# Steps of two batches in a fused attention kernel: one run of small matmuls for a pair's scores and the preceding pair's values

## The chip, the core and the metric

The kernel runs on one core of one Trainium2 chip. The metric is the device time of one execution in microseconds (us); a time of the kernel is the median of several executions. In the profile the engines are PE (TensorE: matmuls; PEld is its loading of weights), DVE (VectorE), ACT (ScalarE), POOL (GpSimd) and SP (SyncE, which issues the DMAs).

## What is computed

The input x has 64 batches of 128 tokens of 512 values, all in float32. The output is x plus an attention block of x:

```python
xn = layernorm(x, g_in)
q = (xn @ Wq).reshape(b, n, H, DH).transpose(0, 2, 1, 3) * scale   # H = 16, DH = 64
k, v = split(xn @ Wkv)                # one key and one value head for all 16 query heads
k, v = one null key and null value ahead of the 128
sim = einsum('bhid,bjd->bhij', q, k) + bias      # a bias for each head, query and key
sim = where(causal_mask, neg, sim); sim = where(mask, sim, neg)
attn = softmax(sim)
out = einsum('bhij,bjd->bhid', attn, v) -> (b, n, 1024)
return x + layernorm(out @ Wo, g_out)
```

## The kernel before, in words

Each engine executes its instructions strictly in the order in which the program writes them (a manual schedule); the order of the calls in the step functions is the order on every engine. An engine that waits at one instruction holds up all behind it.

**Tokens and queries.** Batches come in groups of four (GB). load_x brings a tile of tokens, norm_stats (L265 to L270) takes its mean and variance on DVE and a power on POOL, norm_nmr (L278) one more scalar on DVE, norm_apply (L291) normalizes on ACT; it calls norm_nmr itself, so that scalar stands in DVE's order where norm_apply is called. tokens_T (L315) transposes in blocks on DVE, tokens_out (L324) and tokens_in (L332) send the group through memory into xT. The queries of a group are made by Strassen's scheme: token_sum (L460, POOL) forms four sums of token halves, weight_sum four of weights; for each of four query tiles f, product(g, f, 1) to product(g, f, 7) (L478) do four matmuls each with 256 columns (two instructions a matmul) into PSUM tiles "a", "c" (pool ps_q) and "w" (ps_w). keep (L489) copies a partial sum out of "a" on ACT before the next product is added to it, q_out (L496 on ACT, L499 on DVE) writes a quarter of the queries to qT. kv_mm (L343) and kv_out (L364) make keys and values of a batch; keys_T (L388) and values_spread lay them out by DMA once for each group.

**Attention of a batch.** bias_add (L516, POOL) makes the tile S with bias and mask. The queries are in two halves: the upper 64 see at most 64 keys, the lower 64 see 128. scores (L548) does 64x64 matmuls for a half, scores_add (L564 for two split tiles, L566 for a whole one) adds them to S on DVE, scores_max (L571) takes row maxima on DVE, exps (L580) exponentiates on ACT with the sums of each row, rinv (L597) is a reciprocal on DVE, scale (L601) multiplies on POOL, blocks_T (L616) transposes 32x32 blocks on DVE. values (L645) does 32x64 matmuls, values_out (L662) copies them on ACT to oT.

**Output.** out_mm (L676) multiplies a batch's oT with Wo: eight matmuls of 512 columns. For 28 pairs of batches (1, 2) to (55, 56) Strassen's scheme takes its place: out_sums (L709 to L712) makes four sums on POOL, out_product 1 to 7 (L729) four matmuls each of 256 columns, with copies (out_keep, L741 on DVE and L743 on ACT) and sums (out_part, L750 on ACT and L752 on DVE). The layer norm of a batch is then pair_stats (L758 to L762), pair_pow (L766, POOL), pair_nmr (L773), pair_norm (L783, ACT, into PSUM tile "Y"), pair_gain (L786), pair_residual (L789) and store. Batches outside the pairs (0 and 57 to 63) use out_mm, out_stats and residual.

**Steps.** step(n) is one batch: step_a for even n, step_b for odd n, then region(n), in which PE does the small matmuls: scores of batch n + 2 and values of batch n. Between two regions PE does full-array work: one query tile (seven products), keys and values of one batch, and three or four output products. Queries are made six batches ahead. last_step takes the batches from n = 58 on, which have no more queries to make.

Of the kernel before, what the change touches and what calls it, by code (L numbers as in the profile page):

```python
# [17 lines left out]
def kernel(  # L18
# [113 lines left out]

    def load_res_pair(n):
        for b in (n - 2, n - 1):
            if 1 <= b and not plain(b):
                load_res(b)
# [221 lines left out]
    kvts, vds = {}, {}  # L358

    def kv_out(m, pkv):  # L360
        g, t = divmod(m, GB)
        if t == 0:
            kvts[g] = hp.tile([P, 2, GB, DH], FP, tag="kv", name=f"kvt_{g}", bufs=1)
# [6 lines left out]
        if t == GB - 1:  # L370
            vds[g] = dp.tile([P, GB * DH], FP, tag="vd", name=f"vd_{g}")
            to_tokens(vds[g], kvts[g][:, 1].rearrange("p t d -> p (t d)"))
# [12 lines left out]
    def keys_T(g):  # L385
# [8 lines left out]
        kT[g] = hp.tile([P, NQ, GB, Q], FP, tag="kT", name=f"kT_{g}")  # L394
# [19 lines left out]
    def q_tile(g):  # L414
        qT[g] = gp.tile([P, NF, GB, 2, 2, DH], FP, tag="qT", name=f"qT_{g}")

    def q_part(g, c, lo=0, hi=GB):

        return qT[g][:, c % NF, lo:hi, :, c // NF, :]

    def q_half(c, h):
        if c == 0 and h == 0:
            q_tile(0)
        pq = ps_q.tile([P, HT], FP, tag="ac"[c % 2], name=f"pq_{c}_{h}")
        two = slice(2 * h, 2 * h + 2)
        for kc in (2, 0, 3, 1):
# [8 lines left out]
            q_part(0, c, two.start, two.stop),  # L435
# [55 lines left out]
    def q_out(g, c, toks, tag, name=None):  # L491
        lo = toks.start // N
        o = q_part(g, c, lo, lo + 2)
# [32 lines left out]
    def lower_home(n):  # L526

        tiles = [
            ps_y.tile([P, HE], FP, tag="Y", name=f"lo0_{n}"),
            ps_w.tile([P, HE], FP, tag="w", name=f"lo1_{n}"),  # L530
        ]
        return [t.rearrange("p (f j) -> p f j", f=NF) for t in tiles]

    def scores(b, hf, home=None):
        g, t = divmod(b, GB)
        nk = N if hf == 1 else NL
        split = home is not None
        if not split:
            ps = ps_s.tile([P, 2, NF, N], FP, tag="s", name=f"ps_{b}_{hf}")
            pv = ps.rearrange("p r f j -> p r (f j)")[:, :, 0 : NF * nk].rearrange(  # L540
                "p r (f j) -> p r f j", f=NF
            )
            home = [pv[:, r] for r in range(2)]
        for f in range(NF):
            for r in range(2):
                rows = slice(r * DH, (r + 1) * DH)
                for u in range(2):
                    nc.tensor.matmul(  # L548
                        home[r][u * DH : (u + 1) * DH, f, :],
                        qT[g][rows, f, t, hf, u],  # L550
# [4 lines left out]
        pss[b, hf] = home if split else pv  # L555
# [763 lines left out]
```

## Time and profile before

| | |
|---|---|
| median of 3 executions | 1074.78 us |
| lowest, highest | 1074.32, 1075.43 us |
| the profiled execution | 1079.76 us |
| its span in the profile | 1078.0 us |
| granted clock of TensorE, mean | 0.998 |
| DMA traffic | 105.14 MB, mean 98 GB/s |

The profile shows one execution. A span is the time from its first to its last instruction, and times in rows count from the span's start. In a row of the order of time, the first number is the start in us, the second the time until the end of the last of the xN merged instructions, then engine, line, operation, output tile <- input tiles and shapes; in brackets the idle time of the engine just before it and what ended it. The durations of matmuls overlap (the array is a pipeline), so the spacing of the starts tells more than the durations.

### The profile page before, as it was taken

The page shows a single profiled execution, that of the slowest core. Times are in us where ns is not written, and L with a number is a line of the kernel's source. Part 1 is how long each engine was busy: PE and PEld are TensorE (multiplying, and loading weights), DVE is VectorE, ACT ScalarE, POOL GpSimd, SP SyncE. Part 2 cuts the span into 40 slices and gives each one's busy share as a digit, 9 for nine tenths or more (in the row PEclk, how much of TensorE's full clock was granted, in tenths as well). Part 3 has the DMA queues.
Part 4 walks back from the last instruction along what each step waited for, and adds up shares of the span by engine and source line. Part 5 has one row for each costly group of instructions (what it writes and reads, how often), then busy time and mean ns, then how long its engine had stood idle before and what let it go on. Part 6 is the DMA issues. An engine that isn't in the chain of part 4 may idle for free.

```text
span 1078.0 us, 31342 instructions
## 1 busy us (share of the span) xinstructions
PE 1055.6 (98%) x12292; PEld 884.2 (82%) x12292; DVE 771.3 (72%) x1572; ACT 703.9 (65%) x2826; POOL 702.9 (65%) x520
## 2 busy tenths in 40 slices
PE   7989999999999999999999999999999999999997
PEld 7776888888888888888888888888888888888543
DVE  4767677777777777777777778777777777656772
ACT  3446676676676676676676667667667667657681
POOL 3666767586675767667586675768667576766562
PEclk9999999999999999999999999999999999999999
DMA  6414323423134332323423233341422432211211
GB/s 203 148 38 128 118 82 97 138 73 116 62 99 137 97 109 71 120 84 97 138 79 117 66 120 104 97 136 55 128 71 92 143 97 89 71 41 45 66 60 69
DMA packets 69076, 105.14 MB, mean 98 GB/s; under 512 B 9536, under 2 KB 33728, under 8 KB 67136
## 3 DMA queue, kind: packets, MB, share of 16 engines
q1 hardware_dynamic: 68112, 102.08, 29.9%
q8 instruction: 97, 1.59, 0.6%
q10 hardware_dynamic: 816, 1.05, 0.3%
q14 instruction: 51, 0.42, 0.1%
HBM read 67.45 MB, written 35.65 MB: 96 GB/s over the span
## 4 chain that ended last, share of the span: by engine, by line
PE 91%; DVE 2%; POOL 2%; DMA 2%; ACT 2%; issue 1%; ACTq 0%; SPq 0%; DVEq 0%; POOLq 0%
PE pa L478 19%; PE pyX L729 18%; PE pc L478 10%; PE pyY L729 9%; PE po L645 7%; PE pkv L343 6%; PE ps L548 5%; PE pw L478 5%; PE pyw L729 4%; PE lo L548 3%; PE py L676 3%; PE pq L427 1%; DMA x<-in_x_dram 1%; ACT s L580 1%; POOL s L516 1%
## 5 line engine op out<-in xcount | busy, mean ns | idle before, releaser
L580 ACT ACTIVATE s<-s,nmax 128x65 f32<-128x65 f32 (+1 forms) x1024 | 373.3, 373 | 4.2 <-DVE nmax L571 4.2
L601 POOL TENSOR_TENSOR s<-s,rinv 128x512 f32<-128x512 f32 (+1 forms) x128 | 189.5, 1481 | 178.1 <-DVE rinv L597 171.3
L516 POOL TENSOR_TENSOR s<-biasp,mneg 128x1552 f32<-128x1552 f32 x64 | 206.9, 3233 | 72.6 <-DVE sb L616 69.4
L580 ACT ACTIVATION_READ_ACCUMULATOR s<-s,nmax 128x1 f32 x1024 | 200.9, 196 | 0.0
L662 ACT ACTIVATE oT<-po,nv 128x256 f32<-128x256 f32 x256 | 100.6, 475 | 150.3 <-PE po L645 150.3
L729 PE MATMUL pyX<-wT,oT 128*128 128x256 f32 x672 | 161.7, 383 | 0.0
L729 PEld LDWEIGHTS pyX<-wT,oT 128*128 128x128 f32 x672 | 125.4, 190 | 20.7 <-issue 4.8
L478 PE MATMUL pa<-xS,wq 128*128 128x256 f32 x480 | 123.5, 380 | 1.0 <-ACT ku L489 1.0
L571 DVE TENSOR_REDUCE nmax<-s 128x8 f32<-128x520 f32 (+1 forms) x128 | 122.5, 957 | 2.3
L616 DVE STREAM_TRANSPOSE sb<-s 128x1536 f32<-128x1536 f32 x64 | 113.3, 1770 | 6.6 <-PE po L645 4.3
L478 PEld LDWEIGHTS pa<-xS,wq 128*128 128x128 f32 x480 | 90.9, 190 | 14.2 <-ACT ku L489 1.8
L645 PE MATMUL po<-sb,vr 32*64 32x128 f32 (+1 forms) x4096 | 92.0, 305 | 2.0 <-issue 2.0
L489 ACT COPY ku<-pa 128x256 f32<-128x256 f32 x120 | 44.7, 373 | 70.5 <-PE pa L478 65.5
L645 PEld LDWEIGHTS po<-sb,vr 32*64 32x64 f32 x4096 | 71.1, 130 | 18.2 <-issue 12.2
L566 DVE TENSOR_TENSOR s<-ps,s 128x1024 f32<-128x1024 f32 (+1 forms) x70 | 81.7, 1167 | 2.8 <-PE ps L548 2.7
L709 POOL TENSOR_TENSOR yS<-oT 128x512 f32<-128x512 f32 x28 | 35.7, 1275 | 71.1 <-ACT oT L662 71.1
L564 DVE TENSOR_TENSOR s<-lo,s 128x256 f32<-128x256 f32 x116 | 43.8, 420 | 47.8 <-PE lo L548 47.7
L548 PE MATMUL ps<-kT,qT 64*64 64x128 f32 (+1 forms) x2240 | 72.2, 266 | 1.9 <-DVE s L566 1.9
L343 PE MATMUL pkv<-wkv,xT 128*128 128x128 f32 x512 | 70.4, 281 | 3.5 <-ACT xT L304 2.7
L343 PEld LDWEIGHTS pkv<-wkv,xT 128*128 128x128 f32 x512 | 64.3, 191 | 11.5 <-issue 4.6
L499 DVE TENSOR_TENSOR qT<-pc,ku 128x256 f32<-128x256 f32 x120 | 49.4, 412 | 25.2 <-ACT ku L489 19.0
L291 ACT ACTIVATE x<-x,nmr,rstd 128x512 f32<-128x512 f32 x60 | 48.7, 814 | 28.1 <-DVE nmr L278 25.7
(99 smaller groups left out, 2061.4 us busy)
## 6 DMA issues: line engine op xcount, KB each, us to landing
x<-in_x_dram SPq DMA_DIRECT2D x64, 256.0 KB
res<-in_x_dram SPq DMA_DIRECT2D x64, 256.0 KB
out_dram<-y SPq DMA_DIRECT2D x64, 256.0 KB
xd<-xb SPq DMA_DIRECT2D x14, 1024.0 KB
xT<-xd SPq DMA_DIRECT2D x56, 256.0 KB
vr<-vd SPq DMA_DIRECT2D x64, 128.0 KB
kT<-kd SPq DMA_DIRECT2D x64, 64.0 KB
wo<-in_L_cond_Wo_dram SPq DMA_DIRECT2D x1, 2048.0 KB
```

Source lines behind the costliest of these rows:

```text
L343: nc.tensor.matmul(pkv, xT[g][:, t, kc, :], wkv[:, kc, :], start=(kc == 0), stop=(kc == KC - 1),)
L478: nc.tensor.matmul(prod[tag], w[:, kc, f * P : (f + 1) * P], t[:, :, kc, :], start=(start and kc == 0), stop=(kc == HK - 1), skip_group_ch ...
L516: nc.gpsimd.tensor_tensor(S[b], biasp, mneg[:, t].unsqueeze(1).broadcast_to([P, R8, ROW]), ALU.add,)
L548: nc.tensor.matmul(home[r][u * DH : (u + 1) * DH, f, :], qT[g][rows, f, t, hf, u], kT[g][rows, 0 : nk // Q, t, :], start=True, stop=True,)
L566: nc.vector.tensor_tensor(sv, pv, sv, ALU.add)
L571: nc.vector.tensor_reduce(nmax[b][:, hf], S[b][:, :, WITH_NULL[hf]], AX.X, ALU.max, negate=True)
L580: nc.scalar.activation(row, row, AF.Exp, bias=nmax[b][:, hf, k : k + 1], accum_out=rsum[b][:, hf, k : k + 1],)
L601: nc.gpsimd.tensor_tensor(sv, sv, rinvs.pop((b, hf)).unsqueeze(2).broadcast_to([P, R8, sv.shape[2]]), ALU.mult,)
L616: nc.vector.transpose(sb.rearrange("p j e q -> p e j q"), S[b][:, :, 1 : ROW - 1].rearrange("p e (j k) -> p e j k", k=Q),)
L645: nc.tensor.matmul(po[s][rows, to : to + n], vr[g][quad, j, t, :], sb[quad, slots, r * NF : (r + 1) * NF, :], start=(turn == 0), stop=True ...
L662: nc.scalar.activation(oT[b][:, u * NF : (u + 1) * NF, :].rearrange("p f (s q) -> p s f q", q=Q)[:, blocks], po, AF.Identity, bias=nv2,)
L729: nc.tensor.matmul(prod[key], h[:, c, :], w[:, c, :], start=(start and c == 0), stop=(c == HC - 1), skip_group_check=not start,)
```

## The change

A step now takes a pair of batches (2d and 2d + 1), and it has two parts. turn(d) holds the small matmuls: the scores of pair d, both halves, then the values of pair d - 1. body(d) holds the full-array work: keys and values of two batches, two query tiles f0 and f1, and the seven output products of pair d - 1. The softmax of pair d runs beside body(d), layer norm and residual of the output of pair d - 2 too, and the normalization of two tiles of new tokens. All pairs but the last (62, 63) use Strassen's scheme for the output (31 of 32); queries are made one group, two pairs, ahead. The queries of a group stand in eight tiles (four query tiles by two halves of the group) of one buffer each, instead of two large buffers.

```diff
+    def kv_pair(m):
+        pkv = ps_s.tile([P, 2, DIM], FP, tag="s", name=f"pkv_{m}")
+        for i in range(2):
+            kv_mm(m + i, pkv[:, i, 0:KVN])
+        return pkv
...
-        kT[g] = hp.tile([P, NQ, GB, Q], FP, tag="kT", name=f"kT_{g}")
+        kT[g] = hp.tile([P, NQ, GB, Q], FP, tag="kT", name=f"kT_{g}", bufs=1)
...
-        qT[g] = gp.tile([P, NF, GB, 2, 2, DH], FP, tag="qT", name=f"qT_{g}")
+            qT[g, f, h] = gp.tile(
+                [P, GB // 2, 2, 2, DH], FP, tag=tag, name=f"qT_{g}_{f}_{h}", bufs=1
+            )
...
-        S[b] = sp.tile([P, R8, ROW], FP, tag="s", name=f"s_{b}")
+        S[b] = sp.tile([P, R8, ROW], FP, tag="s", name=f"s_{b}", bufs=3)
...
-    P_LAST = B - 9
+    P_LAST = B - 4
...
     def pair_norm(b):
-        yn[b] = ps_y.tile([P, DIM], FP, tag="Y", name=f"yn_{b}")
+        if b % 2 == 0:
+            yns[b] = ps_s.tile([P, 2, DIM], FP, tag="s", name=f"yn_{b}")
+        yn[b] = yns[b - b % 2][:, b % 2]
...
+    def turn(d):
+        a, b, p = 2 * d, 2 * d + 1, 2 * d - 2
+        if d < PAIRS:
+            scores(a, 0, ((ps_y, "Y"), (ps_w, "w")))
+            scores(b, 0, ((ps_q, "a"), (ps_w, "w")))
+            scores(a, 1)
+            scores(b, 1, ((ps_y, "X"), (ps_q, "c")))
+            scores_add(a, 0)
+            scores_add(b, 0)
+            scores_max(a, 0)
+            scores_add(a, 1)
+            scores_add(b, 1)
+        values_rooms(p)
+        values(p)
+        values(p + 1)
+        if d % 2 and (d + 1) // 2 < NG:
+            mask_neg((d + 1) // 2)
+        if d + 1 < PAIRS:
+            bias_add(a + 2)
+        g = d // 2 + 1
+        if d % 2 == 0 and g < NG:
+            token_sum(g, 1)
+            token_sum(g, 2)
+        if d < PAIRS:
+            exps(a, 0)
+        values_out(p, d == PAIRS)
+
+    def body(d):
+        a, b, p, l = 2 * d, 2 * d + 1, 2 * d - 2, 2 * d - 4
+        g, h = d // 2 + 1, d % 2
+        q, soft = g < NG, 0 < d < PAIRS
+        out, ln = 0 <= p <= P_LAST, 0 <= l <= P_LAST
+        xw = g + 1 < NG
+        m = (g + 1) * GB + 2 * h
+        sums = q and h == 0 and d > 0
+        f0, f1 = 2 * h, 2 * h + 1
...
+            pkv = kv_pair(g * GB + 2 * h)
+        if soft:
+            scores_max(b, 0)
+            rinv(a, 0)
+            scale(a, 0)
+        if ln:
+            pair_stats(l + 1)
+            pair_pow(l + 1)
+        if q:
+            kv_pair_out(g * GB + 2 * h, pkv)
+            if h == 1:
+                keys_T(g)
+                values_spread(g)
...
+            pair_nmr(l)
+            pair_nmr(l + 1)
+        if xw:
+            norm_stats(m)
+            norm_stats(m + 1)
...
+            scores_max(a, 1)
+        if q:
+            product(g, f0, 1, ps_q, "a")
+            keep("a", "p1")
+        if ln:
+            pair_norm(l)
+        if q:
+            product(g, f0, 2, ps_w, "w")
+            q_out(g, f0, 0, "w", "p1")
+        if soft:
+            scores_max(b, 1)
+        if ln:
+            pair_gain(l)
+            pair_residual(l)
+            store(l)
+        if soft:
+            exps(b, 0, 0, 4)
...
+            out_product(p, 1, ps_y, "X")
+            out_keep("X", "yp1", "yp1")
...
+            exps(b, 0, 4, 6)
+        if q:
+            product(g, f0, 5, ps_q, "c")
+            product(g, f0, 6, ps_q, "a", start=False)
+            keep("a", "u2")
+        if ln:
+            pair_norm(l + 1)
+        if soft:
+            exps(b, 0, 6)
+            rinv(b, 0)
+        if out:
+            out_product(p, 2, ps_w, "w")
+            out_part(p, 0, "w", "yp1")
+            out_sum(p, 3)
+        if soft:
+            scale(b, 0)
+        if ln:
+            pair_gain(l + 1)
+        if xw:
+            norm_apply(m)
+        if q:
+            product(g, f0, 7, ps_q, "a", start=False)
+            keep("a", "u3")
+            q_out(g, HC + f0, 1, "c", "u3")
+        if ln:
+            pair_residual(l + 1)
+            store(l + 1)
+        if xw:
+            norm_apply(m + 1)
+            tokens_T(m)
+        if soft:
+            exps(a, 1, 0, 1)
+        if q:
+            product(g, f1, 2, ps_w, "w")
+            product(g, f0, 4, ps_q, "a", start=False)
+            q_out(g, HC + f0, 0, "a")
+            product(g, f0, 3, ps_q, "c", start=False)
+            q_out(g, f0, 1, "c", "u2")
+        if xw:
+            tokens_T(m + 1)
+            if h == 1:
+                tokens_out(g + 1)
+                tokens_in(g + 1)
...
+            exps(a, 1, 1, 4)
+        if q:
+            product(g, f1, 1, ps_q, "a")
+            keep("a", "p1")
+            q_out(g, f1, 0, "w", "p1")
+        if soft:
+            exps(a, 1, 4)
+            rinv(a, 1)
+            scale(a, 1)
+            exps(b, 1, 0, 2)
...
+            out_product(p, 3, ps_y, "Y", start=False)
+            out_part(p, 1, "Y", "yu2")
...
+            out_product(p, 7, ps_y, "X", start=False)
+            out_part(p + 1, 1, "X", "yp5")
+        if soft:
+            blocks_T(b)
+        if q:
+            product(g, f1, 4, ps_q, "a", start=False)
+            q_out(g, HC + f1, 0, "a")
+        if out:
+            out_product(p, 4, ps_y, "X", start=False)
+            out_part(p + 1, 0, "X")
...
-    for n in range(-2, P_LAST + 3):
-        step(n)
-    for n in range(P_LAST + 3, B):
-        last_step(n)
+    body(0)
+    for d in range(1, PAIRS):
+        turn(d)
+        body(d)
+    turn(PAIRS)
+    out_mm(B - 2)
+    body(PAIRS)
```

The rest of body(d) (products 5, 6 and 7 of f1, output products 5 and 6, the remaining exponentials, blocks_T(a), the second bias_add, loads and stores) stands where the lines with "..." are. values_out writes a pair's values with four copies in place of eight. In the start, the softmax of batches 0 and 1 comes before the first body, beside the second half of the queries of group 0.

More of the change, by code (lines that the diff above doesn't have):

```diff
@@ L1080, in step_b @@
+        if soft:
+            rinv(b, 1)
+            scale(b, 1)
+        if q:
+            product(g, f1, 7, ps_q, "a", start=False)
+            keep("a", "u3")
+            q_out(g, HC + f1, 1, "c", "u3")
+        if d + 1 < PAIRS:
+            bias_add(b + 2)
+        if d == 0:
+            for k in range(4):
+                out_weight_sum(k)
+        if out:
             out_product(p, 3, ps_y, "Y", start=False)
             out_part(p, 1, "Y", "yu2")
+        if q:
+            product(g, f1, 3, ps_q, "c", start=False)
+            q_out(g, f1, 1, "c", "u2")
@@ L1082, in step_b @@
+        if out:
+            pair_stats(p)
+            pair_pow(p)
             out_product(p, 7, ps_y, "X", start=False)
             out_part(p + 1, 1, "X", "yp5")
-        if soft_hi:
-            rinv(e, 1)
-            scale(e, 1)
-        if q and f == 3 and n > 1:
-            mask_neg(g)
-        if q:
-            product(g, f, 4, ps_q, "a", start=False)
-            q_out(g, HC + f, lo_t, "a")
-            if f == 3:
-                keys_T(g)
-                values_spread(g)
-        if f == 3 and g + 1 < NG:
-            for k in range(1, 3):
-                token_sum(g + 1, k)
```

572 lines of the change are left out of this document (172 added, 400 removed).

## The prediction

> **What bounds the kernel now.** I read the page first, then the busy times by stretch, then the order of time engine by engine over one steady pair of batches.
>
> ```profile
> span 1078.0 us, 31342 instructions
> PE 1055.6 (98%) x12292; PEld 884.2 (82%) x12292; DVE 771.3 (72%) x1572; ACT 703.9 (65%) x2826; POOL 702.9 (65%) x520
> ...
> 500.57:532.62 32.05, 32.05 (x385) 27.76 (x384) 23.91 (x50) 21.44 (x87) 19.36 (x14) 1.00 0.38 123
> ```
>
> The last row (span, then busy time of PE, PEld, DVE, ACT, POOL, clock, DMA) is one pair of batches: PE has no idle time in 32.05 us, the others 8 to 13 us each. So a pair gets cheaper only through less PE work or fewer changes of tile shape, and dearer through any wait that lands on PE. All that counts is whether PE still finds its inputs in time.
>
> ```profile
> 516.50 1.03 PE L478 MATMUL pa<-xS,wq 128*128 128x256 f32 x4
> 517.46 0.69 PE L548 MATMUL lo<-kT,qT 64*64 64x64 f32 x32
> 517.97 1.06 PE L548 MATMUL ps<-kT,qT 64*64 64x128 f32 x32
> 518.96 1.42 PE L645 MATMUL po<-sb,vr 32*64 32x256 f32 x64
> 520.31 1.99 PE L729 MATMUL pyX<-wT,oT 128*128 128x256 f32 x8
> 522.14 1.05 PE L343 MATMUL pkv<-wkv,xT 128*128 128x128 f32 x8
> 523.03 1.03 PE L478 MATMUL pa<-xT,wq 128*128 128x256 f32 x4
> 523.89 1.03 PE L478 MATMUL pw<-xT,wq 128*128 128x256 f32 x4
> ```
>
> **Run of small tiles.** Start to start, four matmuls of 256 columns take 0.86 (523.03 to 523.89), so eight take 1.72. Before the small tiles the four take 0.96, behind them the eight take 1.83: 0.10 and 0.11 for the changes of shape. One run is 2.85 long (517.46 to 520.31), with two more changes inside it that no row shows alone. The change has one run for two batches and so drops one set: at least 0.2, at most 0.2 plus some 0.5 inside. I take 0.65, since four changes of 0.1 and the drain behind the values lie in it. A pair then costs PE 32.05 - 0.65 = 31.4 if nothing waits; over the 29 steps that have query products, **-19 us** (-6 to -20).
>
> **Step of two batches, laid out.** Time 0 is the first score matmul of a turn. The run takes 5.3 (twice 2.85 less 0.4 of inner changes). Then follow PE's groups as body() writes them: keys and values 1.9 (16 matmuls at 0.11, and the change) to 7.2; products 1 and 2 of the first query tile to 8.05 and 8.9; output product 1 to 10.65; products 5 and 6 to 12.35; output product 2 to 14.1; product 7 to 14.95; product 2 of the second tile to 15.8. Next comes product 4. It adds into the PSUM tile "a", so it waits for keep("a","u3"), a copy on ACT. That copy stands on ACT behind norm_apply(m), which waits for a scalar (nmr) on DVE, which stands there behind pair_gain(l + 1). So I follow DVE.
>
> ```profile
> 502.12 0.69 DVE L571 TENSOR_REDUCE nmax<-s 128x8 f32<-128x520 f32 x1
> 502.73 1.22 DVE L566 TENSOR_TENSOR s<-ps,s 128x1024 f32<-128x1024 f32 x1
> 503.86 1.77 DVE L616 STREAM_TRANSPOSE sb<-s 128x1536 f32<-128x1536 f32 x1
> ...
> 509.20 0.20 DVE L597 RECIPROCAL rinv<-rsum 128x8 f32<-128x8 f32 x1 [1.22 <-ACT s L580]
> ...
> 518.29 0.76 DVE L564 TENSOR_TENSOR s<-lo,s 128x256 f32<-128x256 f32 x2 [1.05 <-PE lo L548]
> ...
> 522.51 0.65 DVE L758 BATCH_NORM_STATS2 sto<-y 128x6 f32<-128x512 f32 x1
> ...
> 523.49 1.22 DVE L571 TENSOR_REDUCE nmax<-s 128x8 f32<-128x1032 f32 x1
> 524.62 0.28 DVE L364 TENSOR_TENSOR kvt<-pkv,nkv 128x128 f32<-128x128 f32 x1
> 525.03 0.42 DVE L499 TENSOR_TENSOR qT<-pw,kp 128x256 f32<-128x256 f32 x1
> 525.37 0.20 DVE L597 RECIPROCAL rinv<-rsum 128x8 f32<-128x8 f32 x1
> ...
> 527.73 0.70 DVE L786 TENSOR_TENSOR yn<-yn,gob 128x512 f32<-128x512 f32 x1 [1.06 <-ACT yn L783]
> 528.46 0.69 DVE L789 TENSOR_TENSOR y<-yn,res 128x512 f32<-128x512 f32 x1
> 529.07 0.20 DVE L773 TENSOR_SCALAR nmro<-mvo,rstdo 128x1 f32<-128x1 f32 x1
> ```
>
> DVE starts 0.83 behind the scores (517.46 to 518.29). In program order: four adds of upper halves 1.4, maximum 0.6, lower add 1.13 (502.73 to 503.86), the other batch's lower add in two halves 1.2 (half of 1024 columns each, with the fixed part twice), its upper maximum 0.6, reciprocal 0.12: 5.9. Statistics of an output batch 0.98 (522.51 to 523.49): 6.9. Then it waits until keys and values leave PE, 7.4. From there nothing but work: keys and values of two batches 0.33, two small scalars 0.2, statistics of two token batches 1.97, lower maximum 1.13 (523.49 to 524.62), query sum 0.34, lower maximum 1.13, pair_gain(l) 0.73, pair_residual(l) 0.69, together 6.5: **13.9**. In odd steps keys_T lies between, 0.4: 14.3.
>
> That residual releases pair_norm(l + 1) on ACT, because both norms now share one PSUM tile, as two norms with one tag did before.
>
> ```profile
> 508.74 0.34 ACT L580 ACTIVATE s<-s,nmax 128x65 f32<-128x65 f32 x1
> ...
> 512.09 1.69 ACT L291 ACTIVATE x<-x,nmr,rstd 128x512 f32<-128x512 f32 x2 [0.61 <-DVE nmr L278]
> 513.69 0.39 ACT L580 ACTIVATE s<-s,nmax 128x129 f32<-128x129 f32 x1
> 514.07 0.39 ACT L580 ACTIVATE s<-s,nmax 128x129 f32<-128x129 f32 x1
> ...
> 526.93 0.77 ACT L783 ACTIVATE yn<-y,nmro,rstdo 128x512 f32<-128x512 f32 x1
> 527.63 0.39 ACT L580 ACTIVATE s<-s,nmax 128x129 f32<-128x129 f32 x1
> ```
>
> **First hole.** From the residual on: norm on ACT 0.70 (526.93 to 527.63), first of two exponentials 0.33, the last one to its reciprocal on DVE 0.46 (508.74 to 509.20), reciprocal 0.12, out_part 0.34, pair_gain(l + 1) 0.63, nmr 0.21, norm_apply(m) 0.80 (two take 1.60, 512.09 to 513.69), the copy 0.37, and some 0.17 for four hand-overs: 4.1. Product 4 starts at 18.05 (odd 18.45), where PE was ready at 15.8: **2.25, odd 2.65**. Bounds: had DVE no backlog, the norm could start at 12.85, half a microsecond behind product 6 with the copy between, and the hole would be 1.15; DVE slower by a tenth makes it 3.4.
>
> **Second hole.** Products 4 and 3 take 1.72, then the second tile's product 1 needs "a" again, freed by q_out on ACT. From the release of product 4: query sum 0.35, pair_residual(l + 1) 0.61, nmr 0.21, norm_apply(m + 1) 0.80, one exponential 0.38 (513.69 to 514.07), the copy 0.37, hand-overs 0.1: 2.8, and so **1.1** more. For the rest of the body the same walk has every other release ahead of PE; the closest, by 0.2, is out_part(p + 1, 1) before output product 4. POOL and the DMAs are not late:
>
> ```profile
> 512.28 3.22 POOL L516 TENSOR_TENSOR s<-biasp,mneg 128x1552 f32<-128x1552 f32 x1
> 514.60 0.33 SPq L324 DMA_DIRECT2D xd<-xb  x1
> 518.57 2.34 SPq L332 DMA_DIRECT2D xT<-xd  x4
> ```
>
> The bias that turn() puts ahead of POOL's scales starts about with the turn and takes 3.2, so the powers that nmr needs are done long before 16. The new tokens' way through memory takes 3.97 to the second issue and 2.34 for that; with some 3 to land they are there 9 us behind their transpose, at about 31, and the next step needs them from 35 on.
>
> Both holes are there when a step has output norms and new tokens: d = 2 to 27, 26 steps, 3.5 on average; d = 1 has 0.8. **+92 us** (57 to 120). The row at 512.09 shows the same chain before, with ACT idle for 0.61 until DVE's nmr; no copy that PE needed stood close behind it there.
>
> **Start and end.**
>
> ```profile
> 52.77 1.03 PE L478 MATMUL pa<-xT,wq 128*128 128x256 f32 x4
> ...
> 998.35 0.69 PE L548 MATMUL lo<-kT,qT 64*64 64x64 f32 x32
> ...
> 1061.74 10.57 PE L676 MATMUL py<-wo,oT 128*128 128x512 f32 x24
> ```
>
> Before, the last steady run starts at 998.35 and 79.65 follow; with 29 pairs of 32.05 that leaves 68.9 in front. After: both first batches' softmax comes before the queries of group 1, which I place at 54 instead of 52.77; body(0) takes 14 of PE work, 3.6 behind norm_apply(8) (its power stands on POOL behind a bias) and 2 at copies: the first turn at 74, **+5** (0 to +9). The end: two steps without queries, bound by softmax. From 3.0 ACT has 16 exponentials of 0.33 and 16 of 0.385, 11.4, four copies of values of some 0.6, two norms and two copies, and is through at 19.4; scale, transpose and the output products that stand behind them on DVE and PE end at 24.6 (20 to 27). Then values and their copies 4, two plain products of 7 each (16 matmuls, where 24 take 10.57), and 6 behind PE as now: 73, **-7** (-16 to +3). Three more pairs by Strassen spare PE 1.6 each, but there PE isn't what ends last.
>
> **Sum.** 1078 + 5 - 19 - 7 + 92 = 1149 us of span. The profiled execution took 1079.76 with a span of 1078.0, the median of three runs is 1074.78, 3.2 under the span; I predict **1146**.
>
> **Rivals.**
>
> *No holes.* If DVE's backlog and the scalars come in time, everything else stands: 1146 - 92 = 1054, faster. For it: each engine has idle time enough in the step. Against it: it isn't the sums but the order; from the keys and values on PE to product 4, DVE and ACT have 10.85 of work in a row where PE has 8.6. It decides at 0.8 of holes per step, where 31.4 + 0.8 gives about the time of before. 10%.
>
> *Half the holes.* pair_norm(l + 1) isn't held up: 1.15 + 1.1 in a step, 1146 - 26 x 1.3 = 1112. 12%.
>
> *Holes and a slower clock.* The trace has a hole of PE after which the granted clock fell.
>
> ```profile
> 1042.23 1.26 PE L548 MATMUL ps<-kT,qT 64*64 64x128 f32 x32 [1.94 <-DVE s L566]
> 24.09 1.16 PE L343 MATMUL pkv<-wkv,xT 128*128 128x128 f32 x8 [2.69 <-ACT xT L304]
> 1043.10:1046.40 3.30, 3.30 (x16) 1.43 (x5) 2.77 (x2) 2.99 (x17) 1.73 (x2) 0.50 0.22 81
> 24.00:28.00 4.00, 3.91 (x30) 3.78 (x31) 1.44 (x5) 1.16 (x3) 0.00 (x0) 1.00 0.01 1
> ```
>
> Behind 1.94 of idle the clock is 0.50 for 3.3 us, behind 2.69 it stays 1.00. So a hole of this size can cost half of some 3.3 us more, 1.65, of which the second hole swallows up to 1.1: 0.6 to 1.65 a step, some 1.0, 26 us if every step is hit: 1172. 22%. [...]
>
> *Merging saves nothing* (the inner changes grow with the run): +19, 1165, within the range.
>
> **Chances.** Forecast as worked out 52%, half the holes 12%, slower clock 22%, no holes 10%, something near before 4%. The range goes from under half the holes to over the slower clock in every step: 1105 to 1185. A measurement of this kernel tells 0.2% from no change. Faster 0.10, same 0.02, slower 0.88.
>
> **What would show it.** Right: PE idle twice in each step, first before product 4 of the first tile (released by the ACT copy ku), then before product 1 of the second (released by the ACT copy qT), 2.2 to 2.7 and about 1.1; ACT idle before the activation of norm_apply, released by DVE nmr; a step of some 35 where it was 32.05, and of 31.4 at d = 28 and 29. Wrong: PE without idle time in the steps and 31.4 throughout; or holes elsewhere, at the scores or values, by a DMA or by POOL; or a granted clock under 1 in the steps.

## The result, and the profile after

The changed kernel takes 1169.02 us (median of 4 runs, 1166.83 to 1171.19) beside 1075.11 for the kernel before; the ratio is 1.087, with an interval of 1.0843 to 1.0897. The profiled execution took 1166.83 with a span of 1165.0. The page of the changed kernel begins so:

```profile
span 1165.0 us, 31181 instructions
...
PE 1062.1 (91%) x12364; PEld 908.6 (78%) x12364; DVE 765.4 (66%) x1605; ACT 685.2 (59%) x2705; POOL 709.1 (61%) x526
```

PE has 6.5 us more of busy time than before and 103 of idle time where it had 22. The busy times by stretch show where (span, then busy time of PE, PEld, DVE, ACT, POOL, granted clock, DMA share, GB/s): the first turn, the steps d = 2 to 27, the steps 28 and 29, and the rest.

```profile
76.58:109.30 32.72, 32.37 (x386) 27.83 (x385) 20.47 (x42) 20.47 (x83) 21.57 (x16) 1.00 0.40 122
109.30:1028.81 919.51, 847.93 (x9986) 730.72 (x9985) 617.78 (x1313) 555.50 (x2184) 568.28 (x417) 0.98 0.29 91
1028.81:1091.71 62.90, 62.90 (x770) 55.67 (x769) 40.94 (x81) 39.69 (x164) 41.62 (x29) 1.00 0.16 52
1091.71:1165.00 73.29, 55.29 (x785) 39.60 (x784) 44.84 (x86) 36.70 (x152) 32.88 (x26) 0.95 0.15 52
```

Steps 28 and 29, without new tokens, are 31.45 each and PE has no idle time in them; the 26 steps before lose 72 us of idle time. One step of each parity (even d, then odd d):

```profile
604.77:639.43 34.66, 31.96 (x386) 27.69 (x385) 23.54 (x50) 20.84 (x83) 24.00 (x18) 1.00 0.16 58
639.43:674.62 35.19, 32.05 (x385) 27.75 (x384) 23.98 (x51) 21.86 (x85) 19.72 (x15) 1.00 0.42 128
```

What PE waited for in the whole span (us in total, times, longest):

```profile
PE pa L508 <- ACT ku L519: 63.5, 28, 3.2
PE pa L508 <- ACT qT L525: 11.0, 18, 0.7
```

And the even step around the holes, engine by engine. On PE the first row is product 2 of the second tile, then product 4, 3, and product 1 of the second tile:

```profile
619.72 1.03 PE L508 MATMUL pw<-xT,wq 128*128 128x256 f32 x4
622.84 1.10 PE L508 MATMUL pa<-xS,wq 128*128 128x256 f32 x4 [2.10 <-ACT ku L519]
623.78 1.03 PE L508 MATMUL pc<-xT,wS 128*128 128x256 f32 x4
625.42 1.13 PE L508 MATMUL pa<-xT,wq 128*128 128x256 f32 x4 [0.61 <-ACT qT L525]
```

```profile
618.87 0.78 ACT L811 ACTIVATE yn<-y,nmro,rstdo 128x512 f32<-128x512 f32 x1 [1.11 <-DVE y L817]
...
621.63 0.81 ACT L286 ACTIVATE x<-x,nmr,rstd 128x512 f32<-128x512 f32 x1 [1.28 <-DVE nmr L273]
622.35 0.35 ACT L519 COPY ku<-pa 128x256 f32<-128x256 f32 x1
623.91 0.81 ACT L286 ACTIVATE x<-x,nmr,rstd 128x512 f32<-128x512 f32 x1 [1.21 <-DVE nmr L273]
...
625.01 0.35 ACT L525 COPY qT<-pa 128x256 f32<-128x256 f32 x1
```

```profile
618.06 0.69 DVE L817 TENSOR_TENSOR y<-yn,res 128x512 f32<-128x512 f32 x1
620.38 0.20 DVE L626 RECIPROCAL rinv<-rsum 128x8 f32<-128x8 f32 x1 [1.63 <-ACT s L609]
...
620.79 0.69 DVE L814 TENSOR_TENSOR yn<-yn,gob 128x512 f32<-128x512 f32 x1
621.39 0.20 DVE L273 TENSOR_SCALAR nmr<-mv,rstd 128x1 f32<-128x1 f32 x1
```

The chain of the prediction stands there link by link: residual(l) on DVE ends at 618.75 and releases pair_norm(l + 1) on ACT. The exponentials behind that norm release the reciprocal on DVE at 620.38, behind which stands the gain of batch l + 1 (620.79), and behind the gain the scalar (621.39). The scalar releases norm_apply(m) at 621.63, and only behind it stands the copy for which product 4 waits. Counted from the first score matmul (604.77), product 4 starts at 18.07. A wait also costs a little more than its idle time: behind these two waits the first two matmuls start 0.29 and 0.32 apart, where the others are 0.22 apart.

**The clock.** Nine of the 26 steps have the lower clock (0.50) for one window of 3.41 us. They are 0.8 to 1.4 longer than the shortest step of their parity; less what had already come late when product 4 started, it is 0.7 to 1.0, about 8 us in all. Two windows of 3.41 us and what follows each:

```profile
195.62:199.03 3.41, 1.31 (x7) 1.07 (x7) 2.27 (x7) 1.17 (x3) 3.36 (x3) 1.00 0.02 5
199.03:202.44 3.41, 3.41 (x9) 2.29 (x8) 1.53 (x3) 2.53 (x10) 0.00 (x0) 0.50 0.63 205
407.24:410.66 3.42, 1.50 (x7) 1.38 (x8) 2.28 (x6) 1.51 (x3) 3.02 (x3) 1.00 0.00 0
410.66:414.07 3.41, 2.80 (x14) 2.14 (x13) 1.61 (x4) 3.31 (x16) 0.00 (x0) 1.00 0.69 247
```

All changes of the granted clock in a trace lie on one grid of 3.413 us: in the changed kernel the lower clock begins at 24.95, 199.03, 304.84 and 444.79, which are 51, 31 and 41 times 3.413 apart. Where PE is idle for 2.10 of one window (3.41 - 1.31), the next is granted 0.50; where a hole of the same kind is cut by the edge of a window so that 1.91 fall into one, it stays 1.00. Over the 14 traces of this study, 37 windows at the full clock, the last window or two of each trace aside, were followed by the lower clock, and the least idle time in one of them was 1.94 (in the kernel before, from 1039.63); of the windows that were not, only one reached 1.94 and the next had 1.91 (the one from 407.24 above). Of the windows already at the lower clock, eight with 0.51 to 1.10 of idle time were followed by another at the lower clock (0.97 in the kernel of "The first step" below, ahead of 71.80), and those that gave the full clock back had at most 0.52. So the holes of 2.1 to 2.5 here are hit or missed by where they fall on the grid.

### The profile page after: what moved, and what is told of

Same layout as the page of the kernel before. It is cut to its first block, busy times and chain, and to the rows that moved or that the text cites. A ratio compares the mean times of both kernels' runs of the same rounds, so it can differ in the third digit from the quotient of the medians.

```text
span 1165.0 us, 31181 instructions
## 1 busy us (share of the span) xinstructions
PE 1062.1 (91%) x12364; PEld 908.6 (78%) x12364; DVE 765.4 (66%) x1605; ACT 685.2 (59%) x2705; POOL 709.1 (61%) x526
## 3 DMA queue, kind: packets, MB, share of 16 engines
q8 instruction: 97, 1.59, 0.5%
## 5 line engine op out<-in xcount | busy, mean ns | idle before, releaser
L630 POOL TENSOR_TENSOR s<-s,rinv 128x1024 f32<-128x1024 f32 (+1 forms) x128 | 189.0, 1476 | 289.6 <-DVE rinv L626 288.8
L508 PE MATMUL pa<-xS,wq 128*128 128x256 f32 x480 | 127.5, 389 | 64.0 <-ACT ku L519 63.5
L757 PEld LDWEIGHTS pyX<-wT,oT 128*128 128x128 f32 x744 | 141.2, 190 | 23.4 <-DVE kyu L769 2.4
L600 DVE TENSOR_REDUCE nmax<-s 128x8 f32<-128x1032 f32 (+1 forms) x128 | 121.7, 952 | 0.1
L525 ACT COPY qT<-pa 128x256 f32<-128x256 f32 x60 | 21.7, 361 | 142.3 <-PE pa L508 142.3
L265 POOL TENSOR_TENSOR rstd<-rstd,nhalf 128x1 f32<-128x1 f32 x64 | 35.3, 552 | 91.3 <-DVE rstd L264 91.3
L626 DVE RECIPROCAL rinv<-rsum 128x8 f32<-128x8 f32 x128 | 25.3, 197 | 90.2 <-ACT s L609 90.2
L508 PE MATMUL pa<-xT,wq 128*128 128x256 f32 x240 | 70.6, 421 | 11.2 <-ACT qT L525 11.0
L740 POOL TENSOR_TENSOR oT<-oT 128x512 f32<-128x512 f32 x62 | 77.3, 1266 | 3.8 <-PE pyw L757 1.4
L700 ACT ACTIVATE oT<-po,nv 128x512 f32<-128x512 f32 x126 | 75.5, 676 | 2.7 <-PE po L677 2.3
L811 ACT ACTIVATE yn<-y,nmro,rstdo 128x512 f32<-128x512 f32 x62 | 48.7, 785 | 38.7 <-DVE y L817 37.4
```

What stands on the lines that cost most here:

```text
L508: nc.tensor.matmul(prod[tag], w[:, kc, f * P : (f + 1) * P], t[:, :, kc, :], start=(start and kc == 0), stop=(kc == HK - 1), skip_group_ch ...
L600: nc.vector.tensor_reduce(nmax[b][:, hf], S[b][:, :, WITH_NULL[hf]], AX.X, ALU.max, negate=True)
L630: nc.gpsimd.tensor_tensor(sv, sv, rinvs.pop((b, hf)).unsqueeze(2).broadcast_to([P, R8, sv.shape[2]]), ALU.mult,)
L700: nc.scalar.activation(to, src, AF.Identity, bias=nv2)
L740: nc.gpsimd.tensor_tensor(o, a, b, op)
L757: nc.tensor.matmul(prod[key], h[:, c, :], w[:, c, :], start=(start and c == 0), stop=(c == HC - 1), skip_group_check=not start,)
```

## The theories, and the kernels that tell them apart

Chain theory: the holes come from the order on ACT and DVE, in which copies that PE waits for stand behind layer norms. Rival: ACT and DVE have too much work in a row between the keys and values and product 4, so that any order loses the time somewhere. Beside these stand the clock, and what was found on the way: PE running out of instructions. All kernels below are the changed kernel with edits; each one's busy times over the steps d = 2 to 27 are one row, to be held against 919.51 with 847.93 of PE busy.

### The scalars early

```diff
+        if xw:
+            norm_nmr(m)
+            norm_nmr(m + 1)
         if ln:
             pair_gain(l)
```

> Only the two scalars norm_nmr(m) and norm_nmr(m + 1) go ahead of pair_gain(l) on DVE; ACT keeps its order. Chain theory (the copy keep u3 stands on ACT behind norm_apply(m), which waits for a scalar behind pair_gain(l + 1)): norm_apply(m) starts right behind the exponentials, 1.28 us earlier (its idle time in the profile of the changed kernel), the first hole shrinks from 2.10 and 2.47 to about 0.8 and 1.2, the second goes, no hole is long enough for the lower clock; a step of some 32.5, span about 1090 (1083 to 1100). Rival, too much work in a row on DVE and ACT whatever its order: the hole only moves, steps stay at 34 to 35, span 1150 to 1165.

One run took 1106.41 (before, on the same chip: 1077.25), span 1104.6.

```profile
107.73:968.96 861.23, 829.20 (x9985) 723.84 (x9984) 615.25 (x1313) 553.37 (x2184) 569.05 (x417) 1.00 0.32 98
```

The first hole is 0.95 (even) and 1.32 (odd), the second is gone, the clock stays at 1.00: steps of 32.64 and 33.04. The chain theory holds. Its total of 1090 is 15 too low: the holes are some 0.15 longer than expected, each costs a restart besides, and the runs of small tiles took 6.8 us more than their shortest, of which more below.

### The copy first

```diff
-        if xw:
-            norm_apply(m)
         if q:
             product(g, f0, 7, ps_q, "a", start=False)
             keep("a", "u3")
+        if xw:
+            norm_apply(m)
+        if q:
             q_out(g, HC + f0, 1, "c", "u3")
```

> Only the order on ACT: the copy keep u3 comes ahead of norm_apply(m) instead of behind it. Chain theory: the copy starts behind the exponentials, the first hole falls to 0.1 to 0.3; but norm_apply(m) and norm_apply(m + 1), still late by DVE, now stand ahead of the copy q_out of tile a, so the second hole grows from 0.6 to some 1.6; a step of some 33.5 and no lower clock, since no hole reaches 1.9; span about 1120 (1108 to 1132). Rival, the hole is bound by PSUM tile a and not by what stands ahead of the copy: the first hole stays above 1.5, span above 1150.

One run took 1125.07, span 1123.3. What PE waited for:

```profile
PE pa L508 <- ACT qT L525: 28.4, 27, 1.1
...
PE pa L508 <- ACT ku L519: 5.3, 14, 0.5
```

The hole at product 4 fell from 63.5 us in all to 5.3, and the one at the second tile grew from 11.0 to 28.4 (1.07 a step, where 1.6 was expected). So it is what stands ahead of the copy that decides, and not the PSUM tile.

### The normalization in a gap of ACT

The scalars early, as in the first of these edits, and norm_apply(m) ahead of pair_norm(l + 1):

```diff
+        if xw:
+            norm_apply(m)
         if ln:
             pair_norm(l + 1)
...
-        if xw:
-            norm_apply(m)
         if q:
             product(g, f0, 7, ps_q, "a", start=False)
```

> Both scalars early as in the first kernel of this row of experiments, and norm_apply(m) ahead of pair_norm(l + 1) on ACT, into the 1.11 us in which ACT waited for pair_residual(l). Chain theory: the copy keep u3 follows the exponentials, first hole 0 to 0.3, second none, a step of 31.5 to 31.8, span 1063 to 1075, so about as fast as the kernel before or up to 1% faster. Rival, what a step loses comes back at the next wait (pair_norm, scale, blocks_T later in the body): steps above 33, span above 1100.

Median 1097.12 (4 runs), ratio to before 1.0177 (1.0156 to 1.0198).

```profile
106.29:955.29 849.00, 834.46 (x9985) 721.27 (x9985) 615.26 (x1313) 554.41 (x2184) 569.14 (x417) 1.00 0.32 99
```

```profile
775.69 1.03 PE L508 MATMUL pw<-xT,wq 128*128 128x256 f32 x4
776.94 1.10 PE L508 MATMUL pa<-xS,wq 128*128 128x256 f32 x4 [0.23 <-ACT ku L519]
778.05 1.13 PE L508 MATMUL pc<-xT,wS 128*128 128x256 f32 x4
```

Steps are 32.19 and 32.65, not 31.5 to 31.8: an idle time of 0.23 in a row stands for 0.39 of delay (1.25 from start to start in place of 0.86), and there is a second wait, too short for a note in brackets, at product 3 (1.11 in place of 0.86), for the sum on DVE that gives tile "c" back and stands there behind pair_gain(l + 1).

### The copy ahead of the second norm as well

```diff
+        if q:
+            product(g, f0, 7, ps_q, "a", start=False)
+            keep("a", "u3")
+            q_out(g, HC + f0, 1, "c", "u3")
         if ln:
             pair_norm(l + 1)
         if soft:
             exps(b, 0, 6)
```

> As the kernel with norm_apply(m) early, and the copy keep u3 on ACT ahead of pair_norm(l + 1) too, with the sum q_out that reads it ahead of pair_gain(l + 1) on DVE. Chain theory: nothing that PE waits for stands behind a layer norm any more; no idle time before products 4 and 3, a step of 31.45 to 31.6 where it was 32.19 (even) and 32.65 (odd); with 5 to 7 us in all in which PE runs out of instructions in the run of small tiles, the span is 1067 (1062 to 1074), 1% faster than before. Rival, the norm that now waits moves the hole to blocks_T and the values of the next turn: steps above 32.3, span above 1085.

Median 1111.88, ratio 1.0327 (1.0305 to 1.0349): slower than the kernel before it.

```profile
106.28:969.15 862.87, 836.21 (x9985) 720.77 (x9985) 617.05 (x1313) 554.88 (x2184) 568.94 (x417) 1.00 0.31 97
```

```profile
387.06 1.03 PE L508 MATMUL pc<-xT,wS 128*128 128x256 f32 x4
388.73 1.13 PE L508 MATMUL pa<-xT,wq 128*128 128x256 f32 x4 [0.65 <-ACT qT L525]
390.17 1.13 PE L508 MATMUL pc<-xS,wS 128*128 128x256 f32 x4 [0.30 <-DVE qT L528]
```

The rival had the size right (steps above 32.3, span above 1085; the span is 1107.9), but not the place, blocks_T and the values: product 4 doesn't wait any more, but products 1 and 5 of the second tile, shown above, do. On ACT the copy for "a" now has a norm, two exponentials, norm_apply(m + 1) and one more exponential between itself and the copy before it:

```profile
385.58 0.37 ACT L519 COPY ku<-pa 128x256 f32<-128x256 f32 x1 [1.51 <-PE pa L508]
385.85 0.79 ACT L811 ACTIVATE yn<-y,nmro,rstdo 128x512 f32<-128x512 f32 x1
...
387.23 0.80 ACT L286 ACTIVATE x<-x,nmr,rstd 128x512 f32<-128x512 f32 x1
387.94 0.39 ACT L609 ACTIVATE s<-s,nmax 128x129 f32<-128x129 f32 x1
388.32 0.35 ACT L525 COPY qT<-pa 128x256 f32<-128x256 f32 x1
```

That is 2.47 by the rows' spacing (385.85 to 388.32), where PE has 1.73 of products. But it may still be order, since these five can also stand behind the copy; the next kernel tries it.

### Every copy first

```diff
+        if q:
+            product(g, f1, 2, ps_w, "w")
+            product(g, f0, 4, ps_q, "a", start=False)
+            q_out(g, HC + f0, 0, "a")
+            product(g, f0, 3, ps_q, "c", start=False)
+            q_out(g, f0, 1, "c", "u2")
         if ln:
             pair_gain(l + 1)
             pair_residual(l + 1)
             store(l + 1)
         if xw:
             norm_apply(m + 1)
             tokens_T(m)
         if soft:
             exps(a, 1, 0, 1)
-        if q:
...
```

> As the kernel with keep u3 ahead of pair_norm(l + 1), and the copies and sums that give tiles a and c back to PE go first at the second place too: q_out of tile a ahead of norm_apply(m + 1) and the exponential of the lower half on ACT, q_out of tile c ahead of pair_gain(l + 1) and pair_residual(l + 1) on DVE. Chain theory: the two waits of 0.65 and 0.31 of the kernel before this (and 0.43 in d = 28 and 29) are gone, PE has no idle time in the steps, 31.45 to 31.6 each but for missing instructions (5 to 9 us in all); span 1069 (1063 to 1076), 0 to 1.2% faster than before. Rival, ACT and DVE have too much work in a row at any order: a hole of 0.5 or more turns up at the next tile (product 1 or 5 of the second query tile, or scores and values), span above 1085.

Median 1081.15 (7 runs), ratio 1.0038 (1.0022 to 1.0054), span 1076.9.

```profile
105.95:940.38 834.43, 826.74 (x9986) 723.99 (x9985) 613.47 (x1313) 545.45 (x2184) 568.60 (x417) 1.00 0.32 100
```

No wait for ACT or DVE is left in the steps. DVE does 613 us of work there and ACT 545, as much as in the changed kernel but for 4 and 10 us; the rival falls, and 85 of the 919.51 us are shown to come from order alone, with what it did to the clock. The steps are still 16.7 us over 26 times 31.45, twice what was expected or more (5 to 9), and the idle time has another name:

```profile
PE po L677 <- issue: 3.6, 7, 1.0
PE pkv L338 <- issue: 1.6, 2, 1.1
PE sc_X L578 <- issue: 1.4, 2, 1.1
```

"Issue" is idle time without anything that PE waited for. Most of it lies in the run of small tiles, which takes 5.09 to its last start where nothing is amiss and up to 7.82 here; over the 26 steps the runs are 13.5 over 5.09 each. Sums for missing instructions are counted in this way below. The page of this kernel gives a hint:

```profile
q8 instruction: 97, 1.59, 0.6%
```

97 packets of 16 KB (1.59 MB in all) stand beside 2 times 12364 instructions of PE, 254.9 to a packet; that these packets bring PE's instructions, about 256 each, is an estimate from the two counts. The run of small tiles has 512 instructions in 5.09 us, two packets by that estimate, and in the trace the two packets of a step come 3.4 to 4.1 us apart. In the longest run (step 14, from 490.38) they start 1.35 and 5.03 behind the run's start and take 1.1 and 1.4; PE stands still from 2.90 to 3.84 and from 6.68 to 7.66:

```profile
494.22 0.43 PE L578 MATMUL sc_c<-kT,qT 64*64 64x128 f32 x3 [0.94 <-issue]
498.04 0.43 PE L677 MATMUL po<-sb,vr 32*64 32x128 f32 x3 [0.98 <-issue]
```

In the three worst steps (14, 16 and 18) each of these stops ends 1.25 to 1.55 behind the end of a packet. That ties them to the packets; the test of it comes two sections further on.

### The run cut in two

The kernel with norm and copy exchanged ("the copy ahead of the second norm"), with the keys and values made in turn(d) and handed to body(d):

```diff
         values(p)
+        if d // 2 + 1 < NG:
+            pkvs[d] = kv_pair((d // 2 + 1) * GB + 2 * (d % 2))
         values(p + 1)
```

> As the kernel without holes, but the keys and values of two batches (16 matmuls of 128 columns) stand between values(p) and values(p + 1), so that the run of small tiles is cut in two and the tile shape changes twice more in each of 29 steps. Theory of the shape changes: 0.1 for each change of shape by the rows, 0.2 to 0.3 a step, span 6 to 9 over the uncut one. Rival, the supply of instructions: the 512 instructions of the uncut run are what PE runs out of, and 16 matmuls in the middle give it time, so that the cut costs nothing or gains up to 3 in all. Second rival, what the prediction took for the whole merging, 0.65 a step: 19 over.

Median 1141.46, ratio 1.06 (1.0584 to 1.0616): 30 us over the uncut one, and no theory had that.

```profile
110.27:999.57 889.30, 845.69 (x9986) 721.16 (x9985) 617.15 (x1313) 550.16 (x2184) 569.88 (x417) 1.00 0.30 94
```

```profile
PE pa L508 <- ACT oT L700: 20.5, 29, 0.7
```

0.71 a step of it is a wait that the cut brought with it: product 1 of the first tile, which needs tile "a" again, now waits for a copy of the values to oT. A step is 1.0 longer on average (889.30 and 862.87 over 26), so 0.3 are left, or 0.5 with the missing instructions that went, for two more changes of shape and the restart behind the wait. The point for the supply of instructions is a different one: from d = 4 to 27 all steps but one (34.47) are 34.14 to 34.19 long. With 16 matmuls of the full array in the middle, PE hardly ever ran out of instructions there (the new wait of 0.7 may help too); in the uncut kernel it lost 5.6 us so.

### The places of instructions shifted

These two take the kernel below under "the first step" and add tiny matmuls at the very start, so that every later instruction of PE stands 112 or 224 places further on:

```diff
+    def shift(k):
+        pb = ps_s.tile([P, P], FP, tag="s", name="shift")
+        for _ in range(k):
+            nc.tensor.matmul(
+                pb[0:32, 0:8], ident[:, 0:32], ident[:, 0:8], start=True, stop=True
+            )
...
-    keep_busy(14)
+    shift(33)
+    keep_busy(9)
```

> As the kernel with the powers early; only the start has 33 tiny matmuls whose result nobody reads and 5 of the 14 matmuls fewer that keep PE busy there, so that every later instruction of PE stands 112 places further on (four for each of 28 more matmuls). In that kernel PE stood still for missing instructions mostly in steps 10 to 18 (1.1 us a step on average) and hardly in 19 to 29 (0.2); the stretches of 16 KB in which instructions come (256 of them) move against a step by some 6 a step, so 112 places are 17 steps. Supply theory: the bad stretch moves out of the steps with queries, steps 2 to 11 are like 19 to 28 were, and the sum over steps 2 to 27 above 31.45 each falls from 16.1 to 3 to 8; span 1066 to 1071, 0.4 to 0.9% faster than before. Rival, the stops come from other traffic at that time (loads and stores of tokens, masks): steps 10 to 18 stay the bad ones, same span within 3.

> The same with 224 places (62 tiny matmuls, 6 fewer of the others): 224 is 32 less than a stretch of 256, five steps the other way. Supply theory: the bad stretch of steps 10 to 18 comes at 15 to 23, the sum over steps 2 to 27 stays at 11 to 17, and the span with it (1073 to 1079). Rival, other traffic: steps 10 to 18 stay the bad ones. A second rival, the tiny matmuls themselves do something at the start: both shifted kernels alike.

112 places: median 1073.58 (12 runs) beside 1077.31 for the kernel before (18 runs), ratio 0.9967 (0.9954 to 0.998). 224 places: 1082.21, ratio 1.0044 (1.0026 to 1.0062).

```profile
109.85:933.62 823.77, 823.65 (x9985) 723.18 (x9984) 613.27 (x1313) 544.94 (x2184) 568.75 (x417) 1.00 0.33 102
```

```profile
107.56:940.97 833.41, 825.39 (x9985) 723.82 (x9984) 613.55 (x1313) 544.74 (x2184) 568.75 (x417) 1.00 0.32 101
```

With 112 places the 26 steps are 6.1 us over 26 times 31.45, without the shift 16.1, with 224 places 15.7. The worst steps are 14, 16 and 18 without the shift (2.5, 2.7 and 1.9 over), 22, 24 and 26 with 224 places (2.5, 2.2 and 2.0), and with 112 no step is over by more than 0.62. So the bad steps move with the places and not with time: supply is the cause, and other traffic falls. So do the tiny matmuls themselves, since the two shifted kernels differ. The bad steps came eight later where five were expected, so a stretch moves by some 4 places a step. The trace counts 768 matmul and weight instructions in a step, three times 256, and 4 (odd) or 6 (even) semaphore instructions of PE besides: counted in instructions, the run of small tiles falls on nearly the same place of the packets in one step as in the next. Step 1 begins 5.1 later with 112 places than without (77.80 against 72.71), in which there is one window at the lower clock, so that the gain in the span is smaller (1069.5 against 1076.1). This is the version that beats both kernels, the one before by 0.3%, clear of the noise but less than the 0.4 to 0.9% expected.

### The clock kept up

14 more matmuls of 128 columns in the first hole, and in a second kernel 5 of 256 columns:

```diff
+    def fill(d, k):
+        pb = ps_y.tile([P, HE], FP, tag="Y", name=f"fill_{d}")
+        for _ in range(k):
+            nc.tensor.matmul(pb, ident, wo[:, 0, 0:HE], start=True, stop=True)
...
+            if 2 <= d <= 27:
+                fill(d, 5)
             product(g, f0, 4, ps_q, "a", start=False)
```

> PE does 14 more matmuls of 128 columns, whose result nobody reads, in the first hole of the steps d = 2 to 27, behind product 2 of the second tile and ahead of product 4 of the first; what product 4 waits for is unchanged. Clock theory (a window of 3.41 us with more than about 1.9 us of idle time on PE halves the clock in the next): no step is clocked down any more, every step is 34.7 or 35.1, the mean clock is above 0.99, and the span falls by some 10 to 12 us to about 1154 (1151 to 1157). Rival, the drops of the clock come by another cause, or cost nothing beside the hole: 1162 to 1170. If the matmuls themselves are in the way (they don't fit into the hole): above 1165.

> The changed kernel with 5 matmuls of 256 columns (1.1 us) in the first hole of steps 2 to 27, whose result nobody reads: a tenth of a per cent more instructions instead of five, and idle time of 1.0 to 1.4 left. Clock theory: no step is followed by the lower clock, all steps 34.7 or 35.1 but for missing instructions; 9 steps at about 1.0 each are gained, median 1160 (1156 to 1164). Rival, the drops cost nothing beside the holes or come by another cause: 1166 to 1171.

The first took 1167.06 in one run, no faster; the second has a median of 1162.31 (1157.48 to 1163.03), ratio 1.0784 (1.0758 to 1.081) where the changed kernel has 1.087.

```profile
111.88:1026.08 914.20, 908.79 (x10714) 805.67 (x10713) 617.78 (x1313) 556.02 (x2184) 568.53 (x417) 1.00 0.30 92
```

```profile
108.50:1023.61 915.11, 892.38 (x10246) 771.21 (x10245) 618.00 (x1313) 556.35 (x2184) 568.94 (x417) 1.00 0.30 92
```

In both no step is followed by the lower clock (1.00 in place of 0.98), and the shortest steps are unchanged (34.66 and 35.13): the holes themselves were not touched. The 26 steps together get 4.4 to 5.3 shorter and not 8, mostly because missing instructions take 6.0 to 6.2 in place of 3.5. (The second kernel has 2.1% more matmuls, not a tenth of a per cent as its expectation says; the first has 5.9%.) With 14 matmuls the rest went at the start, where one more window had the lower clock (first turn at 79.74), in steps 28 and 29 (64.6 in place of 62.9) and in step 30 (26.2 in place of 24.8). The total of the first is therefore no verdict; its steps and the second kernel are.

### The first step

In step 0 PE waits 3.22 for a copy behind norm_apply(8). The kernel "the copy ahead of the second norm" with the normalization of tokens 8 and 9 moved behind product 1 of the second tile (d = 0 alone):

```diff
+        if d == 0:
+            for t in (m, m + 1):
+                norm_apply(t)
+                tokens_T(t)
```

> As the kernel before this, and in step 0 alone the normalization of tokens 8 and 9 goes behind product 1 of the second query tile. In the changed kernel PE waited 3.22 us there for a copy behind norm_apply(8), whose power stands on POOL behind a bias. If that is the cause: the first turn starts some 3.3 earlier (about 71 to 72 from the span's start), and the span is 3 lower, 1064 (1058 to 1071). Rival, the wait moves to the two copies behind it or to the first turn (bias, queries): at most 1 us gained.

Median 1112.58 beside 1111.88: nothing gained.

```profile
69.13 1.70 PE L508 MATMUL pa<-xS,wq 128*128 128x256 f32 x4 [2.11 <-ACT ku L519]
```

The wait moved to the next copy behind the normalization, and it brought the lower clock too, for two windows (1.70 for a group that takes 1.03). The cause was tried from the other side, on "every copy first", with the powers ahead of the bias:

```diff
+    norm_stats(8)
+    norm_stats(9)
     bias_add(2)
     body(0)
```

> As the kernel before this, and the statistics of tokens 8 and 9 stand ahead of the bias on POOL in the first step, so that their powers don't wait for 3.2 us of bias. If that is the cause of the wait of 3.2 in step 0: it falls to 0.5 to 1.0, the first turn is 2 to 3 earlier, the span 2 to 4 lower (1066). Rival, as when the normalization was moved behind the second tile: the time comes back in the same step, at most 1 gained.

Median 1078.26 (10 runs), ratio 1.0014 (1.0002 to 1.0025).

```profile
63.61 1.10 PE L508 MATMUL pa<-xS,wq 128*128 128x256 f32 x4 [1.79 <-ACT ku L519]
```

The wait fell by 1.43, little more than half of what was expected; the first turn starts 1.3 earlier (72.71 against 74.02). So the bias was part of the cause, and 1.79 remains.

## Why the prediction was right, point by point

**Run of small tiles: right.** -0.65 a pair was taken and 31.4 forecast for a step without waits; steps 28 and 29 are 31.45. "Merging saves nothing" is out.

**First hole: right.** Product 4 was to start at 18.05 (even) and 18.45 (odd); it starts at 18.07 and, in the odd steps without another delay, at 18.45. The chain behind it is shown by the rows, and by kernels that take links of it away. No step waits for a DMA, as forecast, though the new tokens take 5.4 us to land (median of the page) where the author's estimate was some 3.

**Second hole: right, too large.** 1.1 forecast; idle time of 0.61 and 0.67, some 0.9 with the restart. Both holes and the restarts make 3.2 (even) and 3.7 (odd) a step by the undisturbed steps, 3.45 on average where 3.5 was taken.

**End and steps 28, 29: right.** 73 and 62.8 forecast, 73.3 and 62.9 measured; the steps without queries 24.8 and 25.2 for 24.6. Part of it is chance: the end holds a window at the lower clock (from 1134.28), which had no term.

**Start: too small.** 74 forecast for the first turn, 76.58 measured. Its wait for norm_apply(8) was taken as 3.6 and is 3.2; one window at the lower clock (from 24.95) accounts for up to 1.7 of the rest. 2.4 of the 2.6 too little lie ahead of the first body, whose keys and values start at 56.38 where 54 was taken; this was not taken apart further.

**"Holes and a slower clock": the step that was missed.** The forecast left it out with 52% beside 22%. Its price of some 1.0 a step was about right (0.7 to 1.0 were paid), but only 9 of 26 steps paid it, for which the prediction had no rule: the windows ahead of the lower clock have 2.01 to 2.82 of idle time in these steps, and no other window more than 1.91. That 1169 lies closer to this rival's 1172 than to 1146 is chance, since the clock gave 8 us of its 26.

**The sum.** The span is 16 over the 1149 of the forecast: 2.7 at the start, 0.5 in step 1, about 8 for the clock, 3.5 for missing instructions in the runs of small tiles (no term of the prediction), 0.9 of other idle time marked "issue" in steps 11 (on DVE) and 12 (on PE, behind the run), 1.3 because a step without waits takes 31.45 and not 31.4, 0.4 at the end, less 1.3 for the holes. The other 7 of the 23 between 1146 and 1169.02 come from the way from span to median: the profiled execution of before was 5 us slower than its other runs, the one of after 2 us faster. The four runs of after have spans of 1165.0 to 1169.4 at clocks of 0.982 to 0.977, the longer the lower; that the grid hits more holes in some than in others would explain it, but only one of them has a trace.

**Rivals.** "No holes" (1054) names the reason that turned out true, that it is the order and not the sums, but this order has the holes; with them gone the kernel takes 1081, not 1054. The span is 1076.9 where this rival would have 1057; 18 of these 20 lie in the steps 2 to 27, most of it missing instructions, which it didn't count, while the start was as forecast (first turn at 74.02). The other 7 are again the way from span to median. "Half the holes" was not tried by itself. Why missing instructions cost 13.5 us in the kernel without holes and 3.5 to 7 in those that have holes and the same instructions stays open: idle time in a step may let the supply get ahead, but no run here tells that.

## What to carry to other kernels

Where engines execute in order, walk from each PSUM tile that the matmuls need back to its copy, and look at what stands ahead of that copy on its engine: copies of 0.35 us that stand behind layer norms, which wait for scalars, cost some 3.5 us a step, and moving them and the scalars to the front gave all of it back with the same work. Move all copies that feed the same stretch at once: one alone handed the wait on to the next. And once the matmul engine waits for nothing, look at idle time marked "issue": here a dense run had 512 instructions in 5.09 us, and where it fell in the packets was worth 10.0 us in 26 steps (16.1 and 6.1 over 26 times 31.45).

## What the runs showed of the hardware

The granted clock changed on a fixed grid of 3.413 us. In the kernel before, 1.94 us of idle time on PE in the window from 1039.63 were followed by 0.50 in the next, and a hole of 2.69 that the edge of a window cuts into 1.06 and 1.63 (at 22.46) by 1.00; in the changed kernel windows at the full clock with 2.01 and more were followed by 0.50, those with 1.91 and less by 1.00. The 24,728 instructions of PE are 254.9 to each of 97 packets of 16 KB, and in "every copy first" the two packets of a step come 3.4 to 4.1 us apart. There PE stood still for 0.94 and 0.98 in a run of 512 small matmul and weight instructions, which takes 5.09 us where nothing is amiss, and 112 places of shift made 26 steps 10.0 us shorter.
